# Where two tables' rows of zeros are stored: ahead of the first stage, or amid layer 0's first blocks

## The chip, the cores and the metric

The kernel runs on 1 core of one Trainium2 chip. The metric is the device time in microseconds; the kernel before was run 14 times. The engines of a core are named as the profile names them: PE (matmul; PEld is its weight load), DVE (vector), ACT (activation), POOL (GpSimd), SP (which here only issues DMAs). SPq is the queue of SP. DMAs that SP and ACT issue are "hardware_dynamic" in the profile, the indirect ones that POOL issues are "software_dynamic"; all of them run on the same 16 DMA engines.

## What is computed

Two layers of a transformer over x, of 4 batches x 1024 tokens x 256 features in fp32, each layer an attention-like part and a mixture of experts, with adaptive layer norms:

```python
mod = (_silu(L0_c) @ L0_wmod).reshape(L0_c.shape[0], 6, 1, -1)
sa, ca, ga, sb, cb, gb = ...
h = _layernorm(x, axis=-1) * (1 + ca) + sa
x = x + ga * _L0_attn_ref(h, L0_attn_queries, L0_attn_combiners)
h = _layernorm(x, axis=-1) * (1 + cb) + sb
x = x + gb * _L0_ffn_ref(h, ...)     # 8 experts, the best 2 of a token, 256 -> 1024 -> 256
# layer 1: the same frame around a fast-weight part and 8 experts of 256 -> 256, the best 2
```

In layer 1's experts a token's result is the weighted sum of two experts' rows, plus a bias.

## The kernel before, in words

**Stages.** Stage 1 (up to about 107 us) loads x, computes layer 0's modulation and attention per batch (`first_half`, `second_half`), routes the tokens of layer 0 and stores the normalised rows to a DRAM table `h_rows`. Stage 2 (about 107 to 625 us) is layer 0's experts. The 64 blocks of 128 (token, expert) pairs and a few more are worked off one after the other: POOL gathers block j's rows (`fetch`, L350), its expert's W1 and W2 with their biases (`weights_in`, 128 rows of 8224 bytes; `weights_out`, 128 rows of 9216 bytes; both L350, skipped row by row where the buffer holds the expert already), PE turns the rows (L1442, pm_x), multiplies by W1 (L1490, p_h), ACT applies bias and relu (L1502), PE multiplies by W2 (L1514, p_y), DVE adds the bias (L1525) and POOL scatters the result to a table (`kept`, L825). There are two buffers for W1 and two for W2, taken in turn. Stage 3 is layer 1: its fast weights (L2198, L2246) and its experts in two groups, "ga" (batches' first 512 tokens) and "gb" (the next 384), and a dense last part.

**The tables.** A block of group ga or gb is stored by SP to the DRAM table `ga_y` or `gb_y`, at row block x 128. Only as many blocks as are nearly always enough (`passed`, all but 3) are computed in the main path; pairs of the rare further blocks point to one more row behind the table, which must hold zeros, so that the first sum adds nothing for them. The rare branch has tables of its own, `ga_rare` and `gb_rare`, whose first row must hold zeros for the same reason. A row is 256 fp32, 1 KB. These four rows are what the change is about. In the kernel before they are written from a tile `none` of 128 partitions x 2 fp32, zeroed by POOL (L2626): each of the four DMAs (L2636) moves 8 bytes from each of 128 partitions.

**The order.** Stage 1's PE, ACT, DVE and POOL work is put in order by a planner (`Plan`, with durations and ranks); SP's DMAs in that stage are placed by the framework as their operands become ready. The loop over layer 0's blocks and layer 1 are ordered by hand or by the planner, with SP included. What is written outside of these ordered parts, like L2626 and L2636, the framework places as early as its operands and buffers allow; the buffer of `none` lies in a pool that opens when stage 1's pool closes. Every engine runs its own instructions strictly in order.

**What the steps touch.** In stage 1 SP issues, in order: four loads of x (L237), five small ones (comb, qT, wr_sb, br_sb, rw_sb, L249), four more loads of x, the closing rows of `h_rows` (L921, L922), the store of the gates (L1355), block 0's W1 (L1366), the load of the first gate, broadcast to all partitions (L1358, `ga0`), and the rest of the first weights and wmod1 (L1366, L1367, L223). `ga0` is needed by DVE for `md` (L1214), the combined head matrix of batch 0; the second half of a batch on PE (L1242) reads md. The four zeroed tiles gd0, gd1, md0, md1 (128 x 2 x 128 fp32) are memset by POOL at L914, and DVE later writes only blocks on their diagonals.

In the loop over layer 0's blocks POOL's order in iteration j is `weights_in(j + 1)`, `kept(j - 2)`, `weights_out(j)`, the fetches, and PE's is block j's W1, the turn of block j + 1, and block j - 1's W2. `once(3)` issues the broadcast of the second gate `gb0` (L1358) on SP.

Of the kernel before, what the change touches and what calls it, by code (L numbers as in the profile page):

```python
# [8 lines left out]
F32 = mybir.dt.float32  # L9
# [10 lines left out]
P = 128  # L20
B, S, D = 4, 1024, 256
NC = S // P
KD = D // P
# [8 lines left out]
RARE = 3  # L32
# [104 lines left out]
def blocks_of(n):  # L137

    return 2 * n + E - 1
# [3 lines left out]
def adaln_d2_kernel(  # L143
# [20 lines left out]
    nc = tc.nc  # L164
# [3 lines left out]
    dram = ctx.enter_context(tc.tile_pool(name="dram", bufs=1, space=DRAM))  # L168
# [721 lines left out]
    def behind(ins, those):  # L890
# [18 lines left out]
    gds, mds = [  # L909
        [pa.tile([P, KD, P], F32, name=f"{x}{i}", bufs=1) for i in range(2)]  # L910
        for x in ("gd", "md")
    ]
    for t in (*gds, *mds):
        nc.gpsimd.memset(t, 0.0)  # L914

    g0 = Pairs(const, pa, "g0", NC * B)
    g0.staged(const, pa)
# [442 lines left out]
    q = plan("SP", 0.1, gates_out, after=rows_done, rank=-0.8, lag=2.2)  # L1360
# [264 lines left out]
    with tc.manual_schedule(engines=ORDERED):  # L1625
# [4 lines left out]
    l1 = ctx.enter_context(tc.tile_pool(name="l1", bufs=1))  # L1630
# [6 lines left out]
    groups = [Pairs(l1, l1, "ga", 4 * B), Pairs(l1, l1, "gb", 3 * B)]  # L1637
# [24 lines left out]
        y=3,  # L1662
# [957 lines left out]

    last_pairs = Pairs(l1, l1, "gc", B)
    lasts = {"decay": [], 0: [], 1: []}
    y_of = [dram.tile([g.passed * P + 1, D], F32, name=f"{g.name}_y") for g in groups]
    rare_of = [dram.tile([1 + RARE * P, D], F32, name=f"{g.name}_rare") for g in groups]
    none = l1.tile([P, KD], F32, name="none")
    nc.gpsimd.memset(none, 0.0)  # L2626
    more_of = l1.tile([P, 1], I32, name="more_of")
    rows_of = [dram.tile([g.n * P + 1, D], F32, name=f"{g.name}_rows") for g in groups]
    vbs = [l1.tile([P, g.n], F32, name=f"{g.name}_vb") for g in groups]
# [1 line left out]
    for g, rows in zip(groups, rows_of):  # L2631
        for k in range(KD):
            nc.sync.dma_start(rows[g.n * P :, k * P : (k + 1) * P], ones[:1, :])
    for g, y, y_rare in zip(groups, y_of, rare_of):
        for rows in (y[g.passed * P :, :], y_rare[:1, :]):
            nc.sync.dma_start(rows.rearrange("a (p k) -> (a p) k", k=KD), none)  # L2636
    for c in range(NC):
        if c in firsts:
            slot, slotT, ts = plan.slot("h1"), plan.slot("hT1"), []
# [29 lines left out]
        g, first = groups[which], 4 * which  # L2669
# [14 lines left out]
        if c in (3, 6):  # L2684
# [18 lines left out]
            for q in range(first, c + 1):  # L2703
# [6 lines left out]
                    lambda b, q=q, first=first: (q - first) * B + b,  # L2710
# [114 lines left out]
```

## Time and profile before

| | us |
|---|---|
| median of 14 runs | 1130.65 |
| lowest, highest | 1122.69, 1133.07 |
| the profiled execution: its own time | 1127.4 |
| its span, first to last instruction | 1125.7 |
| PE busy in the span | 1063.2 (94%) |
| granted TensorE clock, mean | 0.983 |
| `none` memset on POOL, length | 0.12 at 122.55 |
| the four stores of zeros on SP | issued 123.30 to 124.46 |

The span is the time from the first to the last instruction; 1.7 us lie around it. In the chain of work that ended last PE has 80% of the span, so most other engines' idle time costs nothing. A wait in the answers below is an engine's idle time ahead of an instruction, with the work that ended last before it as the releaser. The row of 16 DMA engines' busy share can exceed 1 in a short stretch, because it adds up the times of packets that start in it.

### The profile page before, as it was taken

What the parts mean: (1) busy time and instruction counts of PE and PEld (TensorE: products, weight loads), DVE (VectorE), ACT (ScalarE), POOL (GpSimd) and SP (SyncE); (2) the same over time, 40 slices, a digit from 0 to 9 for tenths busy, and PEclk for the clock granted to TensorE, in tenths of its full rate; (3) what the DMA queues carried; (4) which work ended last, traced back from release to release, by engine and by line L of the source; (5) the groups of instructions that cost most, each with busy time, mean ns of one, the idle gap of its engine ahead of it and who ended that gap; (6) DMA issues with size and microseconds to landing.
All of it is one profiled execution on the core that took longest, in us unless ns stands there. A gap on an engine that the chain in (4) does not pass through costs nothing.

```text
span 1125.7 us, 18440 instructions
## 1 busy us (share of the span) xinstructions
PE 1063.2 (94%) x6037; PEld 826.8 (73%) x6037; DVE 594.4 (53%) x2280; ACT 417.7 (37%) x1137; POOL 416.7 (37%) x478
## 2 busy tenths in 40 slices
PE   8998899999999999999999999999999999888883
PEld 5894798998999999999999466565566575546641
DVE  7786333222222222221165688887977536777566
ACT  5976223233333333333343333432424234242520
POOL 1000456555555555554444010010034331635552
PEclk8999999999999999999999999999999999999996
DMA  9403622757552625352071212211114222333532
GB/s 317 167 27 107 176 80 66 277 176 237 166 175 56 212 55 173 96 174 85 25 254 39 77 50 63 75 57 57 38 41 146 87 71 87 113 96 105 156 118 92
DMA packets 92482, 131.35 MB, mean 117 GB/s; under 512 B 32844, under 2 KB 72277, under 8 KB 87774
## 3 DMA queue, kind: packets, MB, share of 16 engines
q0 software_dynamic: 31584, 68.90, 19.6%
q1 hardware_dynamic: 59694, 59.64, 16.5%
q10 hardware_dynamic: 1104, 1.58, 0.4%
q8 instruction: 51, 0.84, 0.3%
q14 instruction: 49, 0.40, 0.1%
HBM read 204.46 MB, written 29.43 MB: 208 GB/s over the span
## 4 chain that ended last, share of the span: by engine, by line
PE 80%; DVE 9%; DMA 4%; issue 3%; ACT 3%; another core or an unknown queue 1%; DVEq 0%; POOL 0%; SPq 0%; ACTq 0%; POOLq 0%
PE p_h L1490 21%; PE p_y L1514 20%; PE p_u L2198 19%; PE p_f L2246 9%; PE p_e L2506 4%; DMA w<-in_W,g_wrow 2%; PE pm_x L2489 1%; PE pm_counts L778 1%; DMA xg<-h_rows,g_row 1%; ACT xn L1023 1%; ACT h2T L1068 1%; DVE ln_st L997 1%; PE pm_gram L1149 1%; PE pm_b L1090 1%
## 5 line engine op out<-in xcount | busy, mean ns | idle before, releaser
L1502 ACT ACTIVATE hid<-p_h,w 128x128 f32<-128x128 f32 x536 | 152.9, 369 | 316.3 <-issue 218.5
L1514 PE MATMUL p_y<-w,hid 128*128 128x256 f32 x1072 | 245.8, 382 | 4.8 <-issue 4.0
L2198 PE MATMUL p_u<-hT,a 128*128 128x512 f32 x512 | 230.2, 597 | 1.0 <-ACTq L2161 0.9
L1514 PEld LDWEIGHTS p_y<-w,hid 128*128 128x128 f32 x1072 | 198.6, 190 | 30.4 <-issue 5.2
L1490 PEld LDWEIGHTS p_h<-xTq,w 128*128 128x128 f32 x1536 | 179.0, 192 | 2.9 <-DMA w<-in_W,g_wrow 0.4
L1490 PE MATMUL p_h<-xTq,w 128*128 128x128 f32 x1536 | 179.3, 275 | 0.0
L350 POOL DMA_INDIRECT w<-in_W,g_wrow x134 | 135.2, 1009 | 108.7 <-ACT hid L1502 66.7
L2198 PEld LDWEIGHTS p_u<-hT,a 128*128 128x128 f32 x512 | 95.4, 191 | 103.4 <-issue 94.0
L2246 PE MATMUL p_f<-a,hf 128*128 128x256 f32 x512 | 118.9, 385 | 3.0 <-DVE step L2287 3.0
L1525 DVE TENSOR_TENSOR y<-p_y,w 128x256 f32<-128x256 f32 x68 | 28.9, 424 | 174.8 <-PE p_y L1514 140.2
L2246 PEld LDWEIGHTS p_f<-a,hf 128*128 128x128 f32 x512 | 97.0, 192 | 22.6 <-issue 6.4
L825 POOL DMA_INDIRECT y<-y,g_dest x68 | 69.7, 1025 | 110.3 <-DVE g_reached L765 49.0
L2294 POOL TENSOR_TENSOR x_sb<-x_sb,step 128x256 f32<-128x256 f32 x32 | 24.3, 760 | 212.3 <-DVE step L2287 164.2
L791 DVE TENSOR_SCALAR_CACHE_REDUCE g_hits<-pm_counts,g_nth 128x128 f16<-128x128 f32 x68 | 23.7, 348 | 137.9 <-PE pm_counts L778 67.2
L1490 PE MATMUL p_h<-xT,w 128*128 128x128 f32 x608 | 71.4, 276 | 4.2 <-DMA w<-in_W,g_wrow 3.7
L1490 PEld LDWEIGHTS p_h<-xT,w 128*128 128x128 f32 x608 | 70.3, 192 | 5.7 <-issue 4.1
L2210 ACT ACTIVATE hf<-p_u,decay 128x512 f32<-128x512 f32 x56 | 38.2, 684 | 78.1 <-PE p_u L2198 69.0
L2506 PE MATMUL p_e<-ew,xT 128*128 x256 | 65.3, 385 | 1.4 <-issue 1.1
L350 POOL DMA_INDIRECT xg<-h_rows,g_row x20 | 19.7, 987 | 104.7 <-DVE g_own L639 98.5
L2214 DVE SCALAR_TENSOR_TENSOR hf<-p_u,decay,hf 128x512 f32<-128x512 f32 x56 | 41.8, 747 | 25.1 <-PE p_u L2198 7.7
L1861 DVE TENSOR_TENSOR h<-h,mod 128x256 f32<-128x256 f32 x128 | 51.4, 422 | 6.1 <-ACT h L1851 4.1
L2506 PEld LDWEIGHTS p_e<-ew,xT 128*128 128x128 f32 x256 | 44.8, 190 | 10.6 <-issue 5.0
(389 smaller groups left out, 1318.7 us busy)
## 6 DMA issues: line engine op xcount, KB each, us to landing
yg<-y SPq DMA_DIRECT2D x32, 256.0 KB
xTq<-square SPq DMA_DIRECT2D x192, 32.0 KB
ga_y<-y SPq DMA_DIRECT2D x36, 128.0 KB
x_sb<-in_x SPq DMA_DIRECT2D x8, 512.0 KB
h_rows<-xn SPq DMA_DIRECT2D x8, 512.0 KB
hT<-square SPq DMA_DIRECT2D x128, 32.0 KB
out_x<-x_sb SPq DMA_DIRECT2D x7, 512.0 KB
gb_y<-y SPq DMA_DIRECT2D x28, 128.0 KB
```

Source lines behind the costliest of these rows:

```text
L350: return nc.gpsimd.indirect_dma_start(out=dst, out_offset=None, in_=table, in_offset=bass.IndirectOffsetOnAxis(ap=index, axis=0), bounds_c ...
L825: nc.gpsimd.indirect_dma_start(out=table, out_offset=bass.IndirectOffsetOnAxis(ap=dest, axis=0), in_=y, in_offset=None, bounds_check=2 * s ...
L1490: nc.tensor.matmul(p1[:, i, :], lhsT=w1[:, k * H + m * P : k * H + (m + 1) * P], rhs=xT[k], start=(k == 0), stop=(k == KD - 1),)
L1502: nc.scalar.activation(hid[:, m, :], p1[:, i, :], AF.Relu, bias=w1buf[j % 2][:, KD * H + m : KD * H + m + 1],)
L1514: nc.tensor.matmul(p2, lhsT=hid[:, m, :], rhs=w2[:, m * D : (m + 1) * D], start=(m == 0), stop=(m == KH - 1),)
L1525: nc.vector.tensor_tensor(y, p2, w2buf[j % 2][:, KH * D :], ALU.add)
L1861: nc.vector.tensor_tensor(h, h, mods1[(sc, sh)[i]][:, b, :], (ALU.mult, ALU.add)[i])
L2198: nc.tensor.matmul(pu, lhsT=a[:, k, m * P : (m + 1) * P], rhs=made["n1", c, "hT"][:, k, :, :], start=(k == 0), stop=(k == KD - 1),)
L2210: nc.scalar.activation(made[key, m], made[key, m, 0], AF.Silu, scale=decays[c])
L2214: nc.vector.scalar_tensor_tensor(h, made[key, m, 1], decays[c], h, ALU.mult, ALU.mult)
L2246: nc.tensor.matmul(made[key, "p2", b], lhsT=made[key, m][:, b * P : (b + 1) * P], rhs=a1[:, m, :], start=(m == 0), stop=(m == KH - 1),)
L2506: nc.tensor.matmul(made[key, "p2"], lhsT=made[key, "xT"][:, k, :], rhs=ew_flat[:, bass.ds(made[key, "at"] + k * D, D)], start=(k == 0), st ...
```

## The change

The tables `y_of` and `rare_of` are allocated in stage 1's set-up, before `h_rows`, and their rows of zeros are stored there by SP from partition 0 of the zeroed tile md0, one piece of 1 KB for each row. The tile `none`, its memset and its four stores are gone. The sizes of the tables are the same.

```diff
     for t in (*gds, *mds):
         nc.gpsimd.memset(t, 0.0)
+
+    y_of, rare_of = [], []
+    for name, n in (("ga", 4 * B), ("gb", 3 * B)):
+        last = (blocks_of(n) - RARE) * P
+        y_of.append(dram.tile([last + 1, D], F32, name=f"{name}_y"))
+        rare_of.append(dram.tile([1 + RARE * P, D], F32, name=f"{name}_rare"))
+        for row in (y_of[-1][last:, :], rare_of[-1][:1, :]):
+            nc.sync.dma_start(row, mds[0][:1, :, :].rearrange("p k q -> p (k q)"))
...
-    y_of = [dram.tile([g.passed * P + 1, D], F32, name=f"{g.name}_y") for g in groups]
-    rare_of = [dram.tile([1 + RARE * P, D], F32, name=f"{g.name}_rare") for g in groups]
-    none = l1.tile([P, KD], F32, name="none")
-    nc.gpsimd.memset(none, 0.0)
...
-    for g, y, y_rare in zip(groups, y_of, rare_of):
-        for rows in (y[g.passed * P :, :], y_rare[:1, :]):
-            nc.sync.dma_start(rows.rearrange("a (p k) -> (a p) k", k=KD), none)
```

## The prediction

> **What bounds the kernel now.** I read the page first: span 1125.7 us in an execution that took 1127.4, PE busy 94% of it. So an edit is worth what it gives or takes on PE's own chain. Next the waits of PE over the whole run, to see what it waits for at all, and the one around the edited lines.
>
> ```profile
> span 1125.7 us, 18440 instructions
> PE 1063.2 (94%) x6037; PEld 826.8 (73%) x6037; DVE 594.4 (53%) x2280; ACT 417.7 (37%) x1137; POOL 416.7 (37%) x478
> PE p_h L1490 <- DMA w<-in_W,g_wrow: 3.7, 1, 3.7
> PE p_y L1514 <- DMA w<-in_W,g_wrow: 0.7, 1, 0.7
> ```
>
> Only one wait for weights is long: 3.7 us, once. All of layer 0's other weight loads are hidden. The timeline says where, in order of start (the columns: start, length, instruction, idle time before it and its releaser).
>
> ```profile
> 122.55 0.12 POOL L2626 MEMSET none<- 128x2 f32 x1
> 123.30 0.00 SPq L2636 DMA_DIRECT2D ga_y<-none  x1
> 123.30 0.21 SPq L2636 DMA_DIRECT2D ga_rare<-none  x1
> 123.57 0.42 SPq L2636 DMA_DIRECT2D gb_y<-none  x1
> 124.03 0.43 SPq L2636 DMA_DIRECT2D gb_rare<-none  x1
> ...
> 126.41 0.99 POOL L350 DMA_INDIRECT w<-in_W,g_wrow  x1 [3.73 <-ACT hid L1502]
> ...
> 137.23 3.81 PE L1490 MATMUL p_h<-xT,w 128*128 128x128 f32 x32 [3.71 <-DMA w<-in_W,g_wrow]
> ...
> 141.20 0.47 PE L1442 MATMUL pm_x<-ident,xg 128*128 128x128 f32 x2 [0.17 <-DMA xg<-h_rows,g_row]
> ```
>
> The wait comes right behind the edited stores. The weights it waits for (block 3's 1.05 MB of W1) were asked for at 126.41, 2.4 us after the last of the four zero stores was issued, and came 10.8 us later. The stretches of 1 us (the last two columns: busy share of the 16 DMA engines, a value over 1 being packets that overlap, and GB/s) compare this load with block 2's, of the same size, asked for at 118.98:
>
> ```profile
> 122.00:123.00 1.00, 1.00 (x11) 1.00 (x10) 0.00 (x0) 0.00 (x0) 0.67 (x2) 1.00 0.97 395
> 123.00:124.00 1.00, 1.00 (x11) 1.00 (x10) 0.00 (x0) 0.42 (x2) 0.00 (x0) 1.00 0.95 374
> ...
> 128.00:129.00 1.00, 1.00 (x11) 1.00 (x11) 0.00 (x0) 0.94 (x4) 0.74 (x1) 1.00 1.94 82
> 130.00:131.00 1.00, 1.00 (x7) 0.87 (x6) 0.23 (x1) 0.97 (x4) 0.70 (x2) 1.00 1.41 82
> 132.00:133.00 1.00, 1.00 (x7) 0.87 (x6) 0.52 (x3) 0.00 (x0) 0.65 (x1) 1.00 0.82 58
> 135.00:136.00 1.00, 0.00 (x0) 0.00 (x0) 0.00 (x0) 0.00 (x0) 0.69 (x2) 1.00 1.02 395
> ```
>
> Block 2's load moves at 395 and 374 GB/s. Block 3's has its packets open from 128, the engines count as busy (1.94), and yet 82 GB/s pass; at 135 it is back at 395. The DMA view of 128 to 134 gives the size of it, and that of 125 to 128 what went before:
>
> ```profile
> DMA packets 33, 0.27 MB, mean 45 GB/s; under 512 B 0, under 2 KB 0, under 8 KB 0
> q0 software_dynamic: 33, 0.27, 78.1%
> ```
>
> ```profile
> DMA packets 857, 0.36 MB, mean 120 GB/s; under 512 B 608, under 2 KB 825, under 8 KB 857
> ```
>
> 33 packets of 8 KB in 6 us: 0.781 x 16 x 6 / 33 = 2.3 us for one, against 0.97 x 16 / (395/8.2 = 48) = 0.32 us at 122. And 608 pieces under 512 B pass just ahead: 4 rows x 128 pieces of 8 B are 512 of them, all into four 1 KB rows of HBM. I read the slow 6 us as these writes being worked off while the reads wait. That is a reading, not a row: the trace has no record of the memory behind the engines.
>
> **The change part by part.** *Removed at 122.55:* the memset, 0.12 us, POOL then being idle for 3.73 us: nothing. The four issues on SP (0.00 + 0.21 + 0.42 + 0.43): SP's next instruction is at 162.40, waiting for DVE: nothing by themselves.
>
> *Removed with them: the slow 6 us.* Block 2's load was through by 124, 5.0 us after its issue (118.98). Block 3's, issued at 126.41, would be through by 131.4; the load that POOL issues at 194.26 took some 6 us, which gives 132.5. PE ends block 1's p_y at 137.23 - 3.71 = 133.52, so the whole 3.71 us goes at either value. What is late next: block 2's W2 (issued 129.05) follows on the same queue, 1.18 MB at the 420 GB/s of 136 to 141 is 2.8 us, so 134.2 to 135.3; then block 4's rows (issued 130.37), 0.13 MB, by 136. PE wants those rows at 133.52 + 3.81 = 137.3. The 0.17 us before pm_x goes as well. Block 3's W2 is issued at 135.92 behind kept(1), which waits for block 1's output, not for the load, so it does not move; at 6 us it is there at 142, and p_y of block 3 starts at about 133.5 + 3.8 + 0.5 + 3.7 + 3.8 = 145.3. From there on each wait of layer 0 hangs on PE's own progress (a weight buffer is asked for again when ACT has read it), so the gain is kept to the end: -3.88. Bounds: 0 if the slow stretch is not of these stores, -3.88 if it goes whole. I take the whole, since it is nearest to block 2's row, 5 us earlier in the same queue.
>
> A rule of the Trainium skill speaks against this ("DMA: Bandwidth & Descriptors", Queues, rings and completion order): each engine takes turns between its queues packet by packet, so a queue with nothing left takes nothing from the other. The trace has the last small packets at 127.x and the slow reads from 128; by that rule the sum would be 0 for this part. The same page (Specifications) says that writes under 512 B are read, changed and written back, which bears the other way, but it gives no price.
>
> *Added:* four issues on SP ahead of h_rows' rows of ones. The nearest rows are those (L921): 0.60 us for two, so 4 x 0.3 = 1.2 us, from 15.13 on. The source is memset on POOL at 9.44 to 10.00, before SP is there: no wait. But each issue is also a step in a ring of eight: the waits of SP show a DMA that waits for the one eight issues earlier.
>
> ```profile
> SPq L1358 <- DMA gates<-gate_rows: 4.0, 1, 4.0
> SPq L1355 <- DVE gate_rows L338: 1.3, 1, 1.3
> SPq L921 <- DMA qT<-in_qT: 0.5, 1, 0.5
> SPq L237 <- DMA comb<-in_comb: 0.3, 1, 0.3
> ```
>
> The last x load waits for comb, the first row of ones for qT: eight back each time. Four stores more push the rows of ones, g_beyond and the gates' store onto the last four x loads, whose last is through at about 21. So the gates' store slips from 17.47 to about 21.3 (+3.8), W1's first load from 17.76 to 21.6, and the gate's load (22.25) to about 24.6, since without x ahead the store lands quicker than in 4.78 us. The broadcast of the gate ran from 23 to 28 before; now it ends at 30 to 31, behind W1. DVE needs it for md (L1214) at 33.15. Cover 2 to 3 us, so I take 0; bounds 0 and +2, if the load has one engine that lags. The four weight loads and wmod1 end 3 to 4 us later, at 43 at most, and are wanted only beyond 100. DVE's first write of md now also waits until the stores have read md: they land at about 21 behind x, 12 us ahead. That wait costs 0.
>
> Sum: 1127.4 - 3.9 = 1123.5 for the profiled execution. That one is 3.25 us under the median of 14 runs (1130.65), so the median becomes 1126.8.
>
> **The rivals.** *The slow stretch stays.* The gate gb0 is broadcast by SP at 121.89 (512 KB out of four rows of 1 KB), amid the same stretch, and could be what clogs the reads; or the reads just meet a bad moment. For it: its packets end when the reads start. Against it: the same broadcast of ga0 at 22.25 has weight loads at its heels, and 26 to 29 shows 352, 443 and 390 GB/s. The time is then 1130.65 with nothing gained, 1130.5 with the 0.17. The packet-by-packet rule above would make it this case.
>
> *The stage pays it back.* Slower than before: the gate's load lands after the four weight loads instead of after one. These end 3.8 us later than their 36, near 40; md goes from 33.15 to 40 and PE, which has its second half of batch 0 queued behind md, loses up to 7: 1130.65 - 3.9 + 7 = 1133.8. It decides once the gate lands past 33.15 + 3.9 + 2.3 = 39.3. Against it: the gate's load stands second after W1 in program order and waits for the gates' store alone.
>
> *The change does not do what it says:* a row of 1 KB cut into 16 pieces again. 64 pieces where 512 were, at 16 us, beside the x loads: an eighth of the slow 6 us, so 0.8 lost at most; 1127.6.
>
> **How the numbers follow.** Stretch gone: 0.69, of which the stage takes part of it back in some: own range 1124.5 to 1128.5. It stays: 0.20. Payback: 0.07. Left over, such as tables that lie elsewhere in HBM and move other waits: 0.04, mostly slower. The 0.2% that a measurement can tell is 2.3 us. Faster 0.67, same 0.20, slower 0.13. The range takes in the case without gain: 1123.2 to 1131.5.
>
> **What would show it.** Right: no wait of p_h for w at 133; block 3's load at 370 to 430 GB/s from 128; p_h of block 3 at 133.5; SP's gates' store near 21 and md still at 33. Wrong: 82 GB/s at 128 with no small pieces ahead, or md past 35.

## The result, and the profile after

The changed kernel takes 1123.38 us (median of 10 runs, 1122.18 to 1126.39) against 1131.39 (47 runs) for the kernel before beside it: a ratio of 0.9937 [0.992, 0.9954], or -7.1 us [-9.1, -5.2]. The medians lie 8.0 us apart; the means of the same runs, 1123.75 and 1130.87, lie 7.1 apart, as the ratio has it. The forecast was faster, by 3.9 us, at 1126.8 (1123.2 to 1131.5). The sign and the mechanism hold; the gain is larger than the sum. The median lies only 0.2 us inside the range, and below the 1124.5 to 1128.5 that the prediction gave for the case that came true.

The execution that was profiled took 1127.3 us, 3.9 above the changed kernel's median and slower than every execution counted in it, so its span of 1125.6 us, next to 1125.7 before, shows no gain. It has to be read place by place. (The edit moves the lines between its two places by 8: L1490 of the kernel before is L1498 in the changed one.) First the edited place in stage 1, the timeline of SP in the changed kernel (start, length, instruction), and SP's waits up to 40 us (total, times, longest).

```profile
15.15 0.32 SPq L922 DMA_DIRECT2D ga_y<-md  x1
16.09 0.25 SPq L922 DMA_DIRECT2D gb_rare<-md  x1
...
21.88 0.24 SPq L1363 DMA_DIRECT2D gates<-gate_rows  x1
22.17 0.37 SPq L1374 DMA_DIRECT2D w<-in_W  x1
23.27 0.38 SPq L1366 DMA_DIRECT2D ga<-gates  x1
```

```profile
SPq L930 <- DMA x_sb<-in_x: 2.0, 1, 2.0
SPq L1363 <- DMA x_sb<-in_x: 1.1, 1, 1.1
```

The four stores start at 15.15, and what stands behind them in the ring of eight (h_rows' rows, L929 and L930, and the gates' store, L1363) now waits for x loads. The gates' store is issued at 21.88, where it was at 17.47.

Then layer 0's blocks 1 to 3, where the long wait was. The stretches of 1 us of the changed kernel (as before, the last three columns are the granted clock, the DMA engines' share and GB/s), and PE's timeline; its line at 33.35 is stage 1's product that waits for md. The fence behind it has the same product, and the two p_y named below, in the kernel before.

```profile
127.00:128.00 1.00, 1.00 (x12) 0.99 (x11) 0.04 (x1) 0.09 (x1) 0.97 (x1) 1.00 1.03 362
128.00:129.00 1.00, 1.00 (x6) 0.87 (x6) 0.83 (x4) 1.00 (x4) 0.73 (x1) 1.00 0.94 337
```

```profile
33.35 2.02 PE L1250 MATMUL pm_o<-md,h1T 128*128 128x128 f32 x16 [0.77 <-DVE md L1222]
...
127.77 3.67 PE L1522 MATMUL p_y<-w,hid 128*128 128x256 f32 x16
131.27 3.73 PE L1498 MATMUL p_h<-xT,w 128*128 128x128 f32 x32
136.44 0.48 PE L1450 MATMUL pm_x<-ident,xg 128*128 128x128 f32 x2 [1.44 <-DMA xg<-h_rows,g_row]
136.99 3.67 PE L1522 MATMUL p_y<-w,hid 128*128 128x256 f32 x16
```

```profile
33.89 2.02 PE L1242 MATMUL pm_o<-md,h1T 128*128 128x128 f32 x16 [0.69 <-DVE md L1214]
...
129.85 3.67 PE L1514 MATMUL p_y<-w,hid 128*128 128x256 f32 x16
...
141.75 3.67 PE L1514 MATMUL p_y<-w,hid 128*128 128x256 f32 x16
```

With the DMA engines' share at 0.94 to 1.03, 337 to 362 GB/s pass; before, 82 passed at a share of 1.94. Block 3's p_h follows block 1's p_y without a wait. A small wait stands in its place, 1.44 us for block 4's rows. From the start of block 1's p_y to the start of block 2's, PE took 11.90 us before (129.85 to 141.75) and takes 9.22 (127.77 to 136.99). This interval is the measure used below.

What hides the gain in this one execution lies far from the edit, in layer 1. By SP's DMAs there, it leads the profile of before by 3.4 us at 621, by 2.0 at 994, by 1.2 at 1079 and by 0.05 at 1121. In two of the stretches where the lead goes the granted clock is lower: 0.50 between 965 and 970 us (0.82 before) and 0.50 between 1105 and 1115 (0.69 and 0.99 before). A second profile of the changed kernel, below, has 0.70 and then 1.00 and 0.64 there, and ends 2.7 us sooner, so this loss is the execution's, not the change's. That the clock accounts for all of it was not shown: at other times in these stretches it is the kernel before that has the lower one (0.84 against 0.94 at 970 to 975 us).

### The profile page after: what moved, and what is told of

Same layout as the page of the kernel before. It is cut to its first block, busy times and chain, and to the rows that moved or that the text cites. A ratio compares the mean times of both kernels' runs of the same rounds, so it can differ in the third digit from the quotient of the medians.

```text
span 1125.6 us, 18442 instructions
## 1 busy us (share of the span) xinstructions
PE 1067.1 (95%) x6037; PEld 828.8 (74%) x6037; DVE 594.5 (53%) x2280; ACT 416.2 (37%) x1137; POOL 416.3 (37%) x477
## 5 line engine op out<-in xcount | busy, mean ns | idle before, releaser
L1522 PE MATMUL p_y<-w,hid 128*128 128x256 f32 x1072 | 248.5, 385 | 3.4 <-issue 3.3
L1498 PEld LDWEIGHTS p_h<-xTq,w 128*128 128x128 f32 x1536 | 179.1, 192 | 2.5
L1498 PE MATMUL p_h<-xTq,w 128*128 128x128 f32 x1536 | 179.2, 275 | 0.0
L1498 PE MATMUL p_h<-xT,w 128*128 128x128 f32 x608 | 71.8, 277 | 0.4 <-DVE xT L1455 0.4
L1498 PEld LDWEIGHTS p_h<-xT,w 128*128 128x128 f32 x608 | 70.9, 193 | 1.7 <-DVE xT L1455 1.0
```

The costliest lines, as they stand in the source:

```text
L1498: nc.tensor.matmul(p1[:, i, :], lhsT=w1[:, k * H + m * P : k * H + (m + 1) * P], rhs=xT[k], start=(k == 0), stop=(k == KD - 1),)
L1522: nc.tensor.matmul(p2, lhsT=hid[:, m, :], rhs=w2[:, m * D : (m + 1) * D], start=(m == 0), stop=(m == KH - 1),)
```

## The experiments

Three theories were set against each other. A, the forecast's: pieces of 8 bytes, 128 of them into one row of 1 KB, hold up the reads that come behind them. B, its first rival: the broadcast of the gate gb0 holds them up, not the stores. A third, in between: any pieces of 8 bytes do it, wherever they land. The expectations call A also A1 and the third A2, and have three more: C, the gain comes of where the stores stand, or of the new order of stage 1, and not of their size; A', further rows add nothing to the first four; and D, set up after the second profile of the kernel before, that PE's wait costs twice, by its length and by a lower clock behind it. Ratios are to the kernel before, run on the same chip; its medians on the three chips of the experiments lie between 1124.82 and 1130.01 us, so two experiments are compared by their ratios. In the expectations "before" and "after" are the two kernels of the diff.

**The size alone.** Stores at the old place and time, as one piece of 1 KB for each row.

```diff
-    none = l1.tile([P, KD], F32, name="none")
+    none = l1.tile([1, D], F32, name="none")
...
-            nc.sync.dma_start(rows.rearrange("a (p k) -> (a p) k", k=KD), none)
+            nc.sync.dma_start(rows, none)
```

> The kernel before with the four rows of zeros stored at the same place (about 123 us), but each row as one piece of 1 KB from one partition. Theory A (the 512 pieces of 8 bytes hold up the reads behind them): block 3's W1 load moves at 370 to 430 GB/s from about 128 us, PE's wait of 3.7 us for it is gone, the time falls by at least the 3.9 us of the sum (ratio 0.9965 or less); if all of the measured gain is of the pieces, ratio 0.994. Theory B (the gate's broadcast issued at 121.89 clogs the reads): the wait stays, ratio 1.000. Theory C (the gain lies in the new order of stage 1): wait and time as before, ratio 1.000.

1121.09 us, ratio 0.9954 [0.993, 0.9978], or -5.2 us. One of the stretches of 1 us in which block 3's weights come:

```profile
130.00:131.00 1.00, 1.00 (x12) 0.99 (x11) 0.10 (x1) 0.14 (x1) 0.98 (x1) 1.00 1.04 387
```

387 GB/s, no wait for w, and the measured interval is 7.54 us. So the move to stage 1 is not needed for this gain; the size of the pieces at the old place is enough, and C, which expected 1.000 here, falls. The gate's broadcast was still there, which already speaks against B.

**The place alone.** The changed kernel, with its early stores cut into pieces of 8 bytes again.

```diff
-            nc.sync.dma_start(row, mds[0][:1, :, :].rearrange("p k q -> p (k q)"))
+            nc.sync.dma_start(row.rearrange("a (p k) -> (a p) k", k=KD), mds[0][:, 0, :KD])
```

> The changed kernel, the stores ahead of the first stage, but each row in 128 pieces of 8 bytes again. Theory A: no wait of PE at block 3; the slow stretch moves to where the stores land, about 20 to 26 us, onto block 0's first W1 load and the gate's load; the gate has 2 to 3 us of cover, so md (33.15 us before) comes up to 4 us later and the ratio is between 0.994 and 0.998. Theory C (place alone matters, not the size): the same time as the changed kernel, ratio 0.994, and W1's first load at full rate.

1120.80 us, 0.9935 [0.9913, 0.9956], the same as the change. Its timeline of SP and of PE in stage 1:

```profile
23.59 0.24 SPq L1363 DMA_DIRECT2D gates<-gate_rows  x1
...
34.07 2.02 PE L1250 MATMUL pm_o<-md,h1T 128*128 128x128 f32 x16 [0.77 <-DVE md L1222]
```

The small pieces do cost here: SP waits 2.6 us for the last x load in place of 1.1, though no bytes pass from 22 to 24 us, and the gates' store behind that wait goes out 1.7 us later than with pieces of 1 KB (23.59 against 21.88). But what comes behind them has time: md's product starts 0.7 us later (34.07 against 33.35; up to 4 us was expected), and the total doesn't show it. Each half of the change is enough by itself.

**Spread or packed.** The changed kernel, plus four stores of 128 pieces of 8 bytes at the old place, into an unread table: each piece into a row of its own, or 128 pieces into one row.

```diff
+    pad = dram.tile([4 * P, D], F32, name="pad")
+    for q in range(4):
+        nc.sync.dma_start(pad[q * P : (q + 1) * P, :KD], none)                                         # spread
+        nc.sync.dma_start(pad[q : q + 1, :].rearrange("a (p k) -> (a p) k", k=KD), none)   # packed, instead
```

> The changed kernel, and in addition at the old place four stores of 128 pieces of 8 bytes to a table that nobody reads, each piece into a row of 1 KB of its own (512 rows). Theory A1 (pieces into the same few rows of HBM are what is slow): no slow stretch, ratio 0.994 as the changed kernel. Theory A2 (any pieces of 8 bytes are slow): a slow stretch of some 6 us at 126 to 132 us, PE waits 3 to 4 us for block 3's weights, ratio 0.997 to 0.998.

> The changed kernel, and in addition at the old place four stores of 128 pieces of 8 bytes into four whole rows of 1 KB of a table that nobody reads: the old traffic, with the new stage 1. Theory A: under 100 GB/s for some 6 us behind the pieces, PE waits 3 to 4 us for block 3's weights, ratio 0.997 to 0.998 against before, so 3 to 4 us over the changed kernel. Theories B and C: no wait, ratio 0.994.

Spread: 1123.02 us, 0.995 [0.9925, 0.9974]. Packed: 1125.96, 0.9974 [0.995, 0.9999]. The intervals of the two ratios overlap, so the traces decide, by the stretches of 1 us of the spread stores:

```profile
129.00:130.00 1.00, 1.00 (x12) 0.99 (x12) 0.00 (x0) 0.02 (x1) 0.96 (x1) 1.00 0.95 378
```

and of the packed ones, with the packed kernel's PE behind them:

```profile
127.00:128.00 1.00, 1.00 (x12) 1.00 (x11) 0.00 (x0) 0.60 (x3) 0.70 (x1) 1.00 1.42 58
128.00:129.00 1.00, 1.00 (x12) 1.00 (x11) 0.00 (x0) 0.54 (x3) 0.69 (x2) 1.00 1.69 74
```

```profile
134.15 3.81 PE L1498 MATMUL p_h<-xT,w 128*128 128x128 f32 x32 [1.03 <-DVE g_reached L765]
```

The DMA view of 123 to 128 has 768 pieces under 512 bytes in both. With as many pieces, stored from 122.7 us on (spread) and from 122.3 us on (packed), 378 GB/s pass when they go to 512 rows and 58 to 74 (with the busy shares above 1 that the kernel before showed) when they go to four. So it isn't the small piece as such; the third theory falls. The packed stretch is shorter than before's, 4 us and not 6, and the interval only 9.44 us. Why it is shorter here was not settled. PE's wait was to be 3 to 4 us and is 1.03. The profile puts it down to the DVE result g_reached; but in the second profile of the changed kernel p_h starts at 133.09, before that result's 133.94, so it was more likely the weights. The ratio is the expected one all the same, but not by way of this wait: the interval is 1.9 us over 7.54, and the ratio 0.0037 (some 4 us) over the changed kernel's. In this profile a wait of 2.24 us for W2 at 209.58, far from the stores, makes up the rest; whether the other executions have it is not known.

**The rival.** The kernel before, with the broadcast of gb0 four blocks later.

```diff
-        if j == 3:
+        if j == 7:
             gate_in(1, gb0)
```

> The kernel before, with the broadcast of the second gate issued four blocks later (iteration 7 instead of 3), the stores of zeros unchanged. Theory B (the broadcast clogs the reads): PE's wait of 3.7 us is gone, ratio 0.9965. Theory A: the slow stretch stays, under 100 GB/s for 4 to 6 us behind the pieces, the wait stays at 2 to 4 us (the stores may land up to 2 us earlier without the broadcast ahead), ratio 0.998 to 1.000.

1125.15 us, 0.999 [0.997, 1.001]: the same. Its stretch and its wait are still there, without the broadcast:

```profile
128.00:129.00 1.00, 1.00 (x11) 1.00 (x11) 0.00 (x0) 1.00 (x4) 0.88 (x1) 1.00 1.98 82
```

```profile
137.02 5.34 PE L1490 MATMUL p_h<-xT,w 128*128 128x128 f32 x32 [3.38 <-DMA w<-in_W,g_wrow]
```

82 GB/s again: B falls. The last line also holds something that no theory had: 5.34 us for block 3's p_h, which took 3.81 in the profile of before.

**The dose.** The kernel before plus four more packed stores, 1024 pieces of 8 bytes in all.

```diff
+    pad = dram.tile([4, D], F32, name="pad")
+    for q in range(4):
+        nc.sync.dma_start(pad[q : q + 1, :].rearrange("a (p k) -> (a p) k", k=KD), none)
```

> The kernel before, with four more stores of 128 pieces of 8 bytes behind its four, into four whole rows of 1 KB of a table that nobody reads: twice the pieces (1024 into 8 rows). Theory A (pieces into the same row are worked off one after the other while reads wait): the slow stretch gets longer, some 12 us in place of 6, PE's wait for block 3's weights 3.7 + 4 to 6 us, ratio 1.003 to 1.006. Theory A' (only the first rows matter, rows are worked off beside each other): stretch and ratio as before, 1.000. Theory B (the gate's broadcast): as before, 1.000.

1131.52 us, 1.0059 [1.0036, 1.0082], slower by 6.6 us. In its stretches and on its PE:

```profile
128.00:129.00 1.00, 1.00 (x11) 1.00 (x10) 0.00 (x0) 0.34 (x2) 0.69 (x2) 1.00 0.05 8
```

```profile
138.26 6.12 PE L1490 MATMUL p_h<-xT,w 128*128 128x128 f32 x32 [5.34 <-DMA w<-in_W,g_wrow]
```

At 128 only 8 GB/s pass; the slow stretch lasts from 127 to 136, some 9 us for 6, the wait is 5.34, and p_h takes over 6 us. More packed pieces, a longer stop: A' falls. The stretch and the wait are shorter than expected (12 us, 7.7 or more). The profiled execution, at 1129.5 us, is also the fastest of the six; its interval is 2.6 us over the mean of before's three profiles, less than the 6.6 us of the ratio.

**The kernel before, twice more.** Two more profiles of the unchanged kernel show whether the long p_h is its habit.

> The kernel before, unchanged, profiled once more: how far the wait at block 3 varies. If the typical run's wait is longer than the 3.7 us of the profile at hand (the measured gain was 6 to 8 us, the sum 3.9), this one shows 5 to 8 us, perhaps with the granted clock halved behind it; if the rest of the gain lies elsewhere, it shows 3 to 4 us again and a lower clock somewhere else.

> The kernel before, a third profile. Theory D: wait of 3 to 4 us at block 3, then the clock halved for 3.4 us or more and block 3's 32 matmuls at 5 to 6 us; if the halving was rare, 3.7 us as in the first profile.

The executions took 1129.05 and 1129.81 us. PE in the one and in the other, and a stretch of the first:

```profile
136.30 5.44 PE L1490 MATMUL p_h<-xT,w 128*128 128x128 f32 x32 [3.15 <-DMA w<-in_W,g_wrow]
```

```profile
136.24 6.56 PE L1490 MATMUL p_h<-xT,w 128*128 128x128 f32 x32 [3.45 <-DMA w<-in_W,g_wrow]
```

```profile
137.00:138.00 1.00, 1.00 (x7) 1.00 (x7) 0.00 (x0) 0.00 (x0) 0.74 (x1) 0.50 0.99 418
```

The weights flow again (418 GB/s), but the granted clock is 0.50: from 136 to 140 the four stretches have 0.75, 0.50, 0.50 and 0.54, which makes 3.4 us at half rate. In the third profile the wait was 3.45 us, p_h took 6.56, and the same sum gives 6.8 us. The profile that the forecast was made from, with a clock of 1.00 at 137, was the exception.

**Kept busy.** The kernel before with 26 products of 128 columns in fp16 on PE ahead of block 3's p_h, to fill the wait and keep the clock.

```diff
+            if j == 3:
+                pb = psum(ps_1, [P, P], "p1_busy")
+                for _ in range(26):
+                    nc.tensor.matmul(pb, lhsT=ones16, rhs=upto16, start=True, stop=True)
```

> The kernel before, with 26 fp16 matmuls of 128 columns, whose result nobody reads, put on PE ahead of block 3's first matmul with W1: they fill most of PE's wait. Theory D (the wait costs twice: its own 3 to 4 us, and then the clock halved for 3.4 us behind it, under which block 3's 32 matmuls take 5.4 us instead of 3.7): the matmuls behind run in 3.7 to 3.9 us, and the time is up to 1.7 us under before, ratio 0.9985. Without D: no gain, ratio 1.000 to 1.002, as the matmuls take time of their own where the wait is short.

1129.26 us, 0.9995 [0.9973, 1.0017].

```profile
133.26 1.61 PE L1972 MATMUL p_busy<-upto,ones 128*128 128x128 f16 x26
...
137.63 5.43 PE L1490 MATMUL p_h<-xT,w 128*128 128x128 f32 x32 [2.75 <-DMA w<-in_W,g_wrow]
```

A miss: the 26 products took 1.61 us, too few to fill the wait; 2.75 us of it remained, and the clock fell all the same (0.50 from about 138 to 142). That the clock could be kept by work was not shown.

**The changed kernel again, and with a later gate.** A second profile of the changed kernel, and the change together with the gate's broadcast at j == 7 (twice), which might be faster than either.

> The changed kernel again, beside the next one on the same chip. Both theories: ratio 0.994, no wait for weights at block 3, no halved clock behind it.

> The changed kernel with the second gate's broadcast four blocks later. With the slow stretch gone, 512 KB less compete with the weights of blocks 2 and 3: both theories expect no wait of PE at block 3; a gain over the changed kernel only if its 1.4 us of wait for block 4's rows comes from the broadcast: ratio 0.994 (no change) to 0.9925.

> The changed kernel with the second gate's broadcast four blocks later, again, now beside the changed kernel. If the broadcast costs block 4's rows their 1.4 us: 1 to 2 us under the changed kernel. If that wait was one execution's: within 1 us of it.

The changed kernel: 1123.06 us, 0.9934 [0.9905, 0.9962]. With the later gate: 1117.54, 0.9936 [0.991, 0.9961], and 1124.08, 0.9939 [0.9917, 0.9961], each against its own runs of the kernel before. By the ratios the three are equal, so the later gate is worth nothing, and no version faster than the change was found. The second profile's PE has no wait before pm_x:

```profile
133.09 3.73 PE L1498 MATMUL p_h<-xT,w 128*128 128x128 f32 x32
136.66 0.40 PE L1450 MATMUL pm_x<-ident,xg 128*128 128x128 f32 x2
```

The 1.44 us for block 4's rows thus belong to the first execution and not to the change in general. Whether the broadcast had a part in them is open: with the later gate, in the execution that runs in step with the first one (p_h of block 3 at 131.29 beside 131.27), this wait isn't there. The second profile's span is 1122.9 us.

**All together.** The interval from block 1's p_y to block 2's p_y on PE, in each profile:

| kernel | interval, us | wait for w, us | p_h of block 3, us |
|---|---|---|---|
| before, three profiles | 11.90, 12.55, 13.98 | 3.71, 3.15, 3.45 | 3.81, 5.44, 6.56 |
| before, gate later | 12.70 | 3.38 | 5.34 |
| before, PE kept busy (1.6 us of it added work) | 13.62 | 2.75 | 5.43 |
| before, twice the packed stores | 15.44 | 5.34 | 6.12 |
| after, two profiles | 9.22, 7.54 | none | 3.73, 3.73 |
| after plus packed stores | 9.44 | 1.03, by the profile for a DVE result | 3.81 |
| one piece late; small early; after plus spread; after with later gate, twice | 7.54 to 7.55 | none | 3.73 |

## Why the prediction came out as it did

**The slow stretch goes with the stores: right.** At block 3's weights it is there in all six profiles with before's packed stores at the old place, and in that of the packed addition to the changed kernel, and in none of the seven others. That the reads wait *because* the memory works off writes to one row one after the other is still a reading: the runs show that it needs many pieces in few rows, not what happens in the memory. A row is one of the table, 1 KB; pieces at distances other than 8 bytes and 1 KB were not run.

**What the stretch costs: mis-sized, the step that failed.** The sum gave back the wait, 3.71, and 0.17 before pm_x, 3.88 in all. It took for granted that PE goes on after a wait as it went before. In the three profiles of before the interval lies 4.4, 5.0 and 6.4 us above 7.54, a mean of 5.3. Of that the wait is 3.44 us on average, so the forecast had it about right, and 1.54 us is a term that the sum lacked, the clock: block 3's p_h takes 5.3 to 6.6 us behind the wait, where the clock falls, instead of 3.7. The last 0.3 us is mostly an overlap that a wait undoes: without one, p_h starts 0.16 us before the modelled end of the p_y ahead. The clock fell behind the wait in four of the five profiles that have before's stores and no more (in five of six with the doubled stores), and in this place in none of the seven profiles without the stretch. The one profile that the working rested on was the fifth. The forecast compared that execution's time with the median, 3.25 us apart, and carried the gain over unchanged; a reader should have asked there what the slower executions do that this one doesn't. That the forecast's range still holds the result is owed to its width and not to this sum.

The Trainium skill says of this ("TensorE: Matmul & The Clock Gate", The HAM clock gate (the "warmup" mystery)) that PE drops to half rate after at least one idle window of about 3.4 us of a free-running counter, and needs one busy window to come back. The half-rate periods of the traces, 3.4 and 6.8 us, agree with one and two such windows. That a wait of 3.71 us did not bring the clock down is no contradiction: a window that runs freely need not fall whole into it. But waits of 2.75, 3.15 and 3.38 us, shorter than a window, were followed by half rate, which the condition does not give.

**The rest of the gain.** 5.3 us by the interval, and 5.2 by the version that changes the size alone, against a total of 7.1 [5.2, 9.1]. At the start of layer 1 (the first p_u) the changed kernel's two profiles are at 617.95 and 618.29 us, those of before at 621.65, 623.65 and 624.60: again 5.2 us between the means. The other 2 us lie within the interval's reach, and no place for them was found. Stage 1 is not it: its end, by the first p_h, lies at 112.80 to 113.53 before, and at 111.47 and 113.29 after. Nor is layer 1: from the first p_u to the end of the span the five profiles with before's stores and no more take 503.5 to 504.2 us, the seven without the stretch 502.7 to 507.7.

**Added work hidden: right.** The ring of eight was read rightly: the gates' store at 21.88 (forecast: about 21.3), W1 at 22.17 (21.6), the gate's load at 23.27 (24.6), and pm_o with md at 33.35, where it was at 33.89. The later broadcast stayed inside its cover, and the rival in which stage 1 pays the gain back fell. No row was cut into 16 pieces: in the first 60 us the changed kernel moves 10,356 packets and the kernel before 10,348, eight more for the four rows.

**What is late next: right in the second profile, not in the first.** The forecast had block 4's rows there by 136, ahead of PE. The second profile has no wait for them; the first has 1.44 us. That all of layer 0's other weight loads are hidden was not quite so: the prediction's own rows have 0.7 us ahead of a p_y, which lies at 582.71 us, far from the edit.

**The rule against the change.** By the Trainium skill ("DMA: Bandwidth & Descriptors", Queues, rings and completion order) the engines alternate between queues packet by packet. By this rule the prediction would have had the stores' part at 0. The runs decide against it as the whole story: as many pieces, in the same queue and within half a microsecond of the same time, cost nothing when spread and hold up the other queue when packed. So where the pieces land matters, which alternation alone does not give; the traces do not show where the reads are held up.

## What to carry to other kernels

As these runs have it, a row is better written from one partition in one piece; if it must come from many partitions, let it be where no load is needed soon after. A stretch in which the DMA engines count as busy but few bytes pass should be looked at for small packets into few rows just ahead of it. And where an execution is faster than the median by more than its own steps explain, take a second profile before a wait is priced: a wait of PE can cost its length and, behind it, a half-rate clock.

## What the hardware showed that was not expected

- 512 pieces of 8 bytes, 4 KB in all, hold up another queue's reads for 4 to 6 us when they go to four rows (82 GB/s and less), 1024 pieces into eight rows for 9 us (8 GB/s from 128 to 129 us), and 512 not at all when they go to 512 rows (378 GB/s).
- The clock after a wait of PE is not told by the wait's length alone: 3.71 us left it at 1.00, while 2.75, 3.15, 3.38 and 3.45 us were followed by 0.50 for 3.4 to 6.8 us.
- It differs between executions of one kernel at other places too: the first profile of the changed kernel was 3.4 us ahead at 621 us and lost this by its end, in part in stretches at 0.50 (965 to 970 and 1105 to 1115 us).
